# In-degree additions on VectorE at the start of the layers, and the copy of x plus offset written during the encoder

## Chip, core and metric

One core of a Trainium2 chip runs the whole kernel in one launch. The metric is the device time of an execution in microseconds, median of the runs; lower is better. TensorE, VectorE (DVE), ScalarE (ACT) and GpSimd (POOL) each work through their own queue in order; SyncE (SP) issues transfers, and GpSimd and ScalarE issue some of their own.

## What is computed

1250 nodes with 1024 features, 20000 edges sorted by target. First a network with an encoder, three residual graph layers and a decoder, then two mean-aggregating layers:

```python
h = layernorm(x, ln_in_g, ln_in_b)
h = relu(h @ W1 + b1) @ W2 + b2                      # encoder, 1024 -> 512 -> 256
for i in range(3):                                   # residual layers
    z = h + segment_sum(h[src], dst)
    z = relu(z @ Wa[i] + ba[i]) @ Wb[i] + bb[i]
    h = h + relu(layernorm(z, ng[i], nb[i]))
x = _layernorm(x + layernorm(x + decoder(h), out_g, out_b))
deg_inv = 1 / max(in_degree, 1)                      # used by the two layers that follow
h = relu(x @ Ws0 + (segment_sum(x[src]) * deg_inv) @ Wn0 + b0)
out = _layernorm(x + (h @ Ws1 + (segment_sum(h[src]) * deg_inv) @ Wn1 + b1))
```

## The kernel before

The graph becomes a matrix A[source, target] of edge counts, kept in SBUF as 10 blocks of 128 source rows by 1254 targets (1250 and four spare columns), and every `segment_sum` is then a matrix product on TensorE. Most products are done with a high and a low part of each float32 operand (`mm3`, L112 to L115: three matmuls; `split_w` and `relu_split` make the two parts, the high one mostly on ScalarE, the low one on VectorE or GpSimd).

**Encoder (L404 to L572).** Five chunks of two row tiles each (`PCH`, `y_chunk`, `h_rows`). A chunk c has four quarters f of 128 hidden columns, each with 24 matmuls into one PSUM buffer of the tag "ps", of which there are four; two `h_rows` follow a chunk in the same ring. In between stand the transpositions of the next chunk's x tiles (`transpose_x`, L437), whose tiles have the tag "xs" with four buffers, and the edges: groups of five edge tiles make one-hot matrices (`one_hots`), TensorE multiplies them (L344), ScalarE copies the product into a window of A and the product's last column into `carry` (L349, L352), and GpSimd adds the carry to the first column of the next window:

```python
S.activation(A[:, :, dst], pa[g][:, :, :w], AF.Copy)
...
first_col = A[:, :, bass.ds(bases[g - 1][1], 1)]
G.tensor_add(first_col, first_col.bitcast(F32), carry[g - 1])
```

As the windows lie where register values say, ScalarE's copy of a group waits for GpSimd's addition of the group before. When all groups are done, VectorE adds the identity to the ten diagonal blocks of A (L566). On VectorE that stands ahead of `hf` (L483), the encoder's row tiles, and these release the PSUM buffers of `h_rows`.

**Residual layers (L576 to L785).** `agg` multiplies h by A (L638) in three column pieces of 384, 512 and 358 targets; ScalarE and VectorE take the result as `zh` and `zl` (L643, L644); `z1_chunk` multiplies by Wa and its `relu_split` gives `z1h` and `z1l`; `z2_rows` multiplies by Wb, normalizes a row tile (L668 to L675) and writes the new h in two parts, `h0h` on ScalarE (L676) and `h0l` on GpSimd (L677). `load_wab` splits the weights of a layer, with the low part on GpSimd.

Two side jobs run in the layers:

- *In-degrees.* `asum` is the sum of A's ten blocks: five additions on VectorE before the first aggregation (L733 to L735), four on GpSimd after the first layer's rows (L772). `degrees` (L586 to L595) sums it over the partitions in layer 1 and writes the reciprocals to DRAM.
- *x plus offset.* `load_xo` (L717 to L726) loads the decoder's offset row `ob` into all partitions, writes it to all ten tiles of `xo_d` in DRAM (one transfer of 5120 KB, issued by SP), and adds x to it by five accumulating transfers of about 1 MB and one small one, issued by GpSimd. The decoder reads `xo_d` as `vt` (L899).

What sets the order: the head of the encoder, the decoder's rows and the final layers are written out by hand (`manual_schedule`). Elsewhere, in the rest of the encoder and in the layers, a scheduler places the instructions of each engine from the program's order and its own estimates. Waits between engines come from tiles: a tile in a released buffer waits for the last users of that buffer.

Of the kernel before, what the change touches and what calls it, by code (L numbers as in the profile page):

```python
# [10 lines left out]
F32 = mybir.dt.float32  # L11
# [5 lines left out]
ALU = mybir.AluOpType  # L17
# [4 lines left out]
P = 128  # L22
N = 1250
NG = 4
NN = N + NG
NT = 10
D = 1024
# [28 lines left out]
def gz(t):  # L56
    return P if t < NT - 1 else N - (NT - 1) * P + NG
# [7 lines left out]
def tile_gnn(ctx, tc, x, es, vecs, W1, W2, b2, Wa, Wb, bb, ng, nb, Wd1, Wd2, bd2, og, ob,  # L65
             Ws0, Wn0, b0l, Ws1, Wn1, b1l, out):
    nc = tc.nc
    V, S, G, T = nc.vector, nc.scalar, nc.gpsimd, nc.tensor
# [9 lines left out]
    xg_d = dram.tile([NG, D], F32, name="xg_d")  # L78
    x1_d = dram.tile([NT, P, D], F32, name="x1_d")
    h1_d = dram.tile([NT, P, D], F32, name="h1_d")  # L80
    xo_d = dram.tile([NT, P, D], F32, name="xo_d")

    def bcast(ap, n):
        return bass.AP(tensor=ap.tensor, offset=ap.offset, ap=[[0, P], [1, n]])
# [27 lines left out]
    def mm3(ps, a_hi, a_lo, b_hi, b_lo, start, stop, go_on=False):  # L112
        T.matmul(ps, a_hi, b_hi, start=start, stop=False, skip_group_check=go_on)  # L113
        T.matmul(ps, a_hi, b_lo, start=False, stop=False, skip_group_check=go_on)  # L114
        T.matmul(ps, a_lo, b_hi, start=False, stop=stop, skip_group_check=go_on)  # L115

    def pst(name, tag="ps", dt=F32):
        return psp.tile([P, 512], dt, name=name, tag=tag)
# [46 lines left out]
    S1 = tc.alloc_tile_pool(name="S1", bufs=1, reuse_waits="tile")  # L165
# [4 lines left out]
    ne, o = NGR * GT, 2 * NGR * GT  # L170
# [7 lines left out]
    xs = {}  # L178
# [203 lines left out]
    def any_edges():  # L382

        with tc.If(flag > 0):
            acc = Ap.tile([P, NT, AW], F32, name="acc", tag="A")
            V.memset(acc, 0.0)
            scratch = [B1.tile([P, 8 * (PW + 2)], F32, name=f"g{s}", tag=f"h0{s}0", bufs=1) for s in "hl"] + spare
            general_adjacency(tc, psp, acc[:, :, :N], (esrc, est[:, ne:2 * ne]), ident, ones, x, A_g, xg_d, scratch)
            res = Ap.tile([P, NT, AW], F32R, name="A", tag="A")
            nc.sync.dma_start(res.bitcast(F32)[:, :, :NN], A_g)  # L390
        return res
# [6 lines left out]
    def new_h(i):  # L398
        return [[hpool.tile([P, 5, DB], F32R, name=f"h{i}{s}{j}", tag=f"h{s}{j}", bufs=2) for j in range(2)]
                for s in "hl"]  # L400
# [25 lines left out]
    def transpose_x(c, ks=(0, 2, 4, 6)):  # L426
        tiles = PCH[c]
        w = sum(gz(t) for t in tiles)
        if c not in h0:
            h0[c] = new_h0(c)  # L430
        hi, lo = h0[c]
        for k in ks:
            pt = pst("pt").rearrange("p (k c) -> p k c", c=PW)
            for i in range(2):
                for j, t in enumerate(tiles):
                    n = gz(t)
                    T.transpose(pt[:, i, j * P:j * P + n], xs[t][:n, (k + i) * P:(k + i + 1) * P], ident[:n, :n])  # L437
            gs = [vec[:, C_G + k + i:C_G + k + i + 1] for i in range(2)]
            for i, g in enumerate(gs):
                S.activation(hi[:, k + i, :w], pt[:, i, :w], AF.Copy, scale=g)  # L440
            for i, g in enumerate(gs):
                V.scalar_tensor_tensor(lo[:, k + i, :w], pt[:, i, :w], g, hi[:, k + i, :w].bitcast(F32),  # L442
                                       ALU.mult, ALU.subtract)
# [31 lines left out]
    def h_rows(t):  # L475
        n = gz(t)
        o = (t % 2) * P
        ps = pst("ps_h")
        for k in range(4):
            yh, yl = yt[t // 2, k // 2]  # L480
            mm3(ps[:n, :DB], yh[:, k % 2, o:o + n], yl[:, k % 2, o:o + n], W2h[:, k], W2l[:, k], k == 0, k == 3)
        i, j = t // 5, t % 5
        V.tensor_add(hf[i][:n, j], ps[:n, :DB], b2c[:n])  # L483
        S.activation(hh[i][:n, j], hf[i][:n, j], AF.Copy)
        G.tensor_sub(hl[i][:n, j], hf[i][:n, j], hh[i][:n, j].bitcast(F32))
# [57 lines left out]
        load_W2()  # L543
    for f in range(4):
        V.tensor_add(b1c[:, f:f + 1], first[f][:, PW:PW + 1], vec[:, C_B1 + f:C_B1 + f + 1])
    NC = len(PCH)
    SLOTS = 13
    for c in range(NC):
        if c == 1:
            A = any_edges()  # L550
        for f in range(4):
            slot = 4 * (c - 1) + f
            y_chunk(c, f, -(-(ET - n_ed) // (SLOTS - slot)) if 0 <= slot < SLOTS else 0)
            if f == 0 and c > 0:
                for t in PCH[c - 1]:
                    h_rows(t)
            if 0 < c < NC - 1:
                transpose_x(c + 1, (2 * f,))
# [3 lines left out]
            if slot == SLOTS - 1:  # L562
# [4 lines left out]
                with tc.If(flag > 0):  # L567
                    nc.sync.dma_start(A.bitcast(F32)[:, :, :NN], A_g)
    for t in PCH[NC - 1]:
        h_rows(t)  # L570
    B1.release()
    S1.release()  # L572

# [2 lines left out]
    asum = WD2.tile([P, NN], F32, name="asum", tag="wd2_3")  # L576
    C3 = tc.alloc_tile_pool(name="C3", bufs=1, reuse_waits="tile")
# [36 lines left out]
    def begin_layer(i):  # L614
        ngc, nbc = (B2.tile([P, DB], F32, name=nm_, tag=nm_, bufs=1) for nm_ in ("ngc", "nbc"))
        bbr = wraw()[0:1, :DB]
        bbl = wraw()[0:1, :DB]
        nc.sync.dma_start(bbr, bass.AP(tensor=bb.tensor, offset=bb.offset + i * DB, ap=[[DB, 1], [1, DB]]))
        split_w(bbr, bbc[0:1], bbl)
        nc.sync.dma_start(bbc[1:2].bitcast(F32), bbl)  # L620
        nc.sync.dma_start(ngc, bcast(ng[i], DB))
        loads["nb"] = nc.sync.dma_start(nbc, bcast(nb[i], DB))
        z = new_z(("zh", "zl")) + new_z(("z1h", "z1l")) if i else z_first + new_z(("z1h", "z1l"))
        L[i].update(vecs=(bbc, ngc, nbc), z=z)

    def new_z(names):
        return [[B2.tile([P, NN], F32R, name=f"{nm_}{k}", tag=f"{nm_}{k}") for k in range(2)] for nm_ in names]
# [18 lines left out]
    def z1_chunk(i, c):  # L646
        c0, w = CL[c]
        cs = slice(c0, c0 + w)
        zh, zl, z1h, z1l = L[i]["z"]
        wh, wl = L[i]["w"]  # L650
        for f in range(2):
            ps = pst("ps_z1")
            for k in range(2):
                mm3(ps[:, :w], wh[:, k, f * P:(f + 1) * P], wl[:, k, f * P:(f + 1) * P],
                    zh[k][:, cs], zl[k][:, cs], k == 0, k == 1)
            bias = vec[:, C_BA + 2 * i + f:C_BA + 2 * i + f + 1]
            relu_split(ps, w, bias, z1h[f][:, cs], z1l[f][:, cs], B2, 512, f == 0)
# [56 lines left out]
            V.tensor_sub(d[64:], d[64:], bdo[64:, fs])  # L714
            S.activation(bdo[64:, fs], d[64:], AF.Copy)

    def load_xo():  # L717

        o = C3.tile([P, D], F32, name="o", tag="wt")
        nc.sync.dma_start(o, bcast(ob, D))  # L720
        nc.sync.dma_start(xo_d.rearrange("t p f -> p t f"), o.unsqueeze(1).broadcast_to([P, NT, D]))
        rows = xo_d.rearrange("t p f -> (t p) f")
        for t in range(0, NT, 2):
            r0, r1 = t * P, min(N, t * P + 2 * P)
            G.dma_start(rows[r0:r1], x[r0:r1], accum_op=ALU.add, max_dma_last_dim=4 * D)
        G.dma_start(rows[N:NN], xg_d, accum_op=ALU.add, max_dma_last_dim=4 * D)  # L726

    z_first = new_z(("zh", "zl"))
    load_wab(1)
    load_wab(0)  # L730
    begin_layer(0)
    load_xo()
    V.tensor_add(asum, A[:, 0, :NN].bitcast(F32), A[:, 1, :NN].bitcast(F32))  # L733
    for t in range(2, 6):
        V.tensor_add(asum[:gz(t)], asum[:gz(t)], A[:gz(t), t, :NN].bitcast(F32))  # L735
    for t0, t1 in ((0, 8), (8, NT)):
        agg(0, 0, t0, t1)
# [1 line left out]
    for i in range(3):  # L739
        nh, nl = new_h(i)  # L740

        def rows(*ts):
            for t in ts:
                z2_rows(i, t, nh, nl)

        z1_chunk(i, 0)
        z1_chunk(i, 1)
        rows(0, 1)
        agg(i, 2, 0, 5, (0,))
        rows(2, 3)  # L750
        agg(i, 2, 5, NT, (0,))
        if i == 1:
            degrees()
            load_Wd2(2)
        rows(4)
        agg(i, 2, 0, NT, (1,))
        rows(5, 6)
        if i == 2:
            break
        z1_chunk(i, 2)  # L760
        hh, hl = nh, nl
        agg(i + 1, 0, 0, 4)
        rows(7, 8, 9)
        begin_layer(i + 1)
        agg(i + 1, 1, 0, 4)
        agg(i + 1, 0, 4, 7)
        agg(i + 1, 1, 4, 7)
        if i == 0:
            with tc.issue_after(loads["nb"].ins):
                nc.sync.dma_start(A_d, A.bitcast(F32)[:, :, :NN])  # L770
            for t in range(6, NT):
                G.tensor_add(asum[:gz(t)], asum[:gz(t)], A[:gz(t), t, :NN].bitcast(F32))  # L772
            load_wab(2)
            for k in range(2):
                load_Wd2(k)
        else:
            load_Wd1()
            load_Wd2(3)
            load_bdo()
        agg(i + 1, 0, 7, NT)  # L780
        agg(i + 1, 1, 7, NT)
# [352 lines left out]
    A, loaded = {}, []  # L1134
# [178 lines left out]
    for i in range(2):  # L1313
# [3 lines left out]
        rows = h1_d if last else x1_d  # L1317
# [339 lines left out]
```

## Time and profile before

| | us |
|---|---|
| median of three runs | 932.36 (931.75 to 932.67) |
| the profiled execution, device time | 934.92 |
| its span in the profile | 933.1 |
| encoder ends, first aggregation starts | 128.3 |
| first aggregation ends, first product with Wa | 144.5 |
| layer 1's first zl | 188.97 |
| matmuls of the degrees | 203.6 |

The lines of a timeline give the start, the duration (of all instructions that were merged, with their count at the end), the engine, the line of the source, the operation, the tile written and those read with their shapes, and in brackets how long the engine was idle before and what released it. "issue" means that no releaser shows. A table of stretches gives, for each stretch, the busy time of each engine with its number of instructions, the granted clock of TensorE (1.00 is full), the busy share of the transfer engines, and GB/s. A matmul's record overlaps the next one, so its pitch is shorter than its duration.

### The profile page before, as it was taken

The page shows a single profiled execution, that of the slowest core. Times are in us where ns is not written, and L with a number is a line of the kernel's source. Part 1 is how long each engine was busy: PE and PEld are TensorE (multiplying, and loading weights), DVE is VectorE, ACT ScalarE, POOL GpSimd, SP SyncE. Part 2 cuts the span into 40 slices and gives each one's busy share as a digit, 9 for nine tenths or more (in the row PEclk, how much of TensorE's full clock was granted, in tenths as well). Part 3 has the DMA queues.
Part 4 walks back from the last instruction along what each step waited for, and adds up shares of the span by engine and source line. Part 5 has one row for each costly group of instructions (what it writes and reads, how often), then busy time and mean ns, then how long its engine had stood idle before and what let it go on. Part 6 is the DMA issues. An engine that isn't in the chain of part 4 may idle for free.

```text
span 933.1 us, 13196 instructions
## 1 busy us (share of the span) xinstructions
PE 898.3 (96%) x4753; PEld 790.0 (85%) x4759; DVE 646.2 (69%) x1269; ACT 393.7 (42%) x760; POOL 138.0 (15%) x160
## 2 busy tenths in 40 slices
PE   6789998999899999999999999999999999999997
PEld 4689998898887778999988888889999988888885
DVE  8878668676796774585677576455566786777785
ACT  3567523344566884111233345553211333333454
POOL 3467546526120000000000000000000000000000
PEclk9989999999999999999999999999999999999999
DMA  6300038973213739987452235446996722222214
GB/s 228 128 24 19 2 118 238 228 283 95 71 66 114 237 129 335 377 294 270 153 190 79 80 117 176 154 173 216 310 313 215 229 84 77 81 77 79 79 47 174
DMA packets 84163, 148.37 MB, mean 159 GB/s; under 512 B 8280, under 2 KB 31851, under 8 KB 84090
## 3 DMA queue, kind: packets, MB, share of 16 engines
q1 hardware_dynamic: 77062, 126.90, 40.1%
q0 software_dynamic: 2816, 10.27, 4.5%
q10 hardware_dynamic: 4212, 10.27, 2.9%
q8 instruction: 39, 0.64, 0.3%
q14 instruction: 34, 0.28, 0.1%
HBM read 103.35 MB, written 49.21 MB: 163 GB/s over the span
## 4 chain that ended last, share of the span: by engine, by line
PE 85%; DVE 6%; ACT 1%; DMA 1%; issue 1%; POOL 1%; ACTq 0%; POOLq 0%; DVEq 0%; SPq 0%
PE ps_A L1210 20%; PE ps_m L115 14%; PE ps_m L113 14%; PE ps_m L114 14%; PE ps_z L638 4%; PE ps_dd L113 2%; PE ps_dd L115 2%; PE ps_dd L114 2%; PE pa L344 2%; PE ps_y L113 2%; PE ps_y L114 2%; PE ps_y L115 1%; DVE z L673 1%; DVE hf L675 1%; PE pt L962 1%
## 5 line engine op out<-in xcount | busy, mean ns | idle before, releaser
L113 PE MATMUL ps_m<-w,th 128*128 128x512 f32 x520 | 204.0, 392 | 0.0
L115 PE MATMUL ps_m<-w,th 128*128 128x512 f32 x520 | 202.6, 390 | 0.0
L114 PE MATMUL ps_m<-w,th 128*128 128x512 f32 x520 | 202.3, 389 | 0.0
L1210 PE MATMUL ps_A<-A,qh 128*128 128x418 f32 (+1 forms) x480 | 170.6, 355 | 0.0
L1210 PE MATMUL ps_A<-A,ql 128*128 128x418 f32 (+1 forms) x480 | 169.9, 354 | 0.0
L115 PEld LDWEIGHTS ps_m<-w,th 128*128 128x128 f32 x520 | 97.6, 188 | 20.7
L114 PEld LDWEIGHTS ps_m<-w,th 128*128 128x128 f32 x520 | 97.7, 188 | 20.0
L113 PEld LDWEIGHTS ps_m<-w,th 128*128 128x128 f32 x520 | 97.6, 188 | 19.6
L1210 PEld LDWEIGHTS ps_A<-A,ql 128*128 128x128 f32 (+1 forms) x480 | 90.7, 189 | 1.9
L125 DVE TENSOR_TENSOR w<-stage,w 128x512 fp32r<-128x512 f32 x65 | 44.7, 691 | 67.9 <-ACT w L124 67.5
L1210 PEld LDWEIGHTS ps_A<-A,qh 128*128 128x128 f32 (+1 forms) x480 | 90.3, 188 | 1.4
L124 ACT ACTIVATE w<-stage 128x512 fp32r<-128x512 f32 x65 | 40.7, 629 | 118.7 <-PE ps_m L115 74.6
L1215 DVE TENSOR_TENSOR MT<-ps_A,dgb 128x418 f32<-128x418 f32 x48 | 25.5, 587 | 64.2 <-PE ps_A L1210 64.2
L1171 ACT ACTIVATE qh<-qraw 128x1280 fp32r<-128x1280 f32 (+3 forms) x28 | 21.5, 809 | 105.1 <-PE ps_A L1210 87.5
L113 PE MATMUL ps_y<-h0h,w1h 128*128 128x256 f32 (+2 forms) x160 | 54.9, 343 | 0.0
L125 DVE TENSOR_TENSOR w<-wraw,w 128x512 fp32r<-128x512 f32 x39 | 26.9, 689 | 32.8 <-ACT w L124 30.7
L114 PE MATMUL ps_y<-h0l,w1h 128*128 128x256 f32 (+2 forms) x160 | 46.4, 290 | 1.0 <-DVE h0l L442 1.0
L1299 DVE TENSOR_TENSOR c<-ps_m,c 128x512 f32<-128x512 f32 (+1 forms) x65 | 40.9, 683 | 8.8 <-PE ps_m L115 8.7
L115 PE MATMUL ps_y<-h0h,w1l 128*128 128x256 f32 (+2 forms) x160 | 46.1, 288 | 0.0
L1040 ACT ACTIVATE th<-XT 128x640 fp32r<-128x640 f32 x48 | 34.2, 725 | 20.5 <-DVE MT L1215 20.5
L124 ACT ACTIVATE w<-wraw 128x512 fp32r<-128x512 f32 x39 | 24.5, 629 | 41.9 <-PE ps_m L115 21.3
L328 POOL TENSOR_SCALAR Q<-iq,q 128x260 bf16<-128x260 f16 x31 | 37.9, 1223 | 14.6 <-PE pa L344 13.9
(306 smaller groups left out, 1897.9 us busy)
## 6 DMA issues: line engine op xcount, KB each, us to landing
A<-A_d SPq DMA_DIRECT2D x20, 627.0 KB
w_d<-stage SPq DMA_DIRECT2D x43, 256.0 KB
stage<-w_d SPq DMA_DIRECT2D x43, 256.0 KB
stage<-in_l_W_neigh_dram SPq DMA_DIRECT2D x42, 256.0 KB
stage<-in_l_W_self_dram SPq DMA_DIRECT2D x28, 256.0 KB
A_d<-A SPq DMA_DIRECT2D x1, 6270.0 KB
wraw<-in_l_W_neigh_dram SPq DMA_DIRECT2D x22, 256.0 KB
w_d<-wraw SPq DMA_DIRECT2D x21, 256.0 KB
```

Of the source, the lines that this page charges most:

```text
L113: T.matmul(ps, a_hi, b_hi, start=start, stop=False, skip_group_check=go_on)
L114: T.matmul(ps, a_hi, b_lo, start=False, stop=False, skip_group_check=go_on)
L115: T.matmul(ps, a_lo, b_hi, start=False, stop=stop, skip_group_check=go_on)
L124: S.activation(hi, raw, AF.Copy)
L125: return eng.tensor_sub(lo, raw, hi.bitcast(F32))
L328: G.tensor_scalar(q[:, 0], iq[:, :m], q4[:, g:g + 1], None, ALU.is_equal)
L638: T.matmul(ps[:, :w], hx[t // 5][:n, t % 5, f * P:(f + 1) * P], A[:n, t, c0:c0 + w], start=(t == 0 and s == 0), stop=(t == NT - 1 and s == 1))
L1040: S.activation(hi, src, AF.Copy)
L1171: S.activation(q[0][:, t0:t1], raw[:, t0:t1], AF.Copy)
L1210: T.matmul(pss[j][c][:, :w], qs[j][s][:n, t], A_of(t)[:n, c0:c0 + w], start=start and s == 0, stop=stop and s == 1)
L1215: V.tensor_mul(MT[:, f, c0:c0 + w], pss[j][c][:, :w], dgb[:, c0:c0 + w])
L1299: V.tensor_add(c, ps[:n], c if last or M in (6, 7) else c11[:n, t])
```

## The change

`load_xo` moves from the start of the residual layers to the end of the encoder, right after the last `h_rows`; the tile of the offset takes an x buffer (tag "xs") in place of one of the decoder's. The additions for blocks 6 to 9 of `asum` move from GpSimd, after layer 0's rows, to VectorE, in one row with the other five before the first aggregation.

```diff
@@ -543,6 +543,17 @@
         load_W2()
     for f in range(4):
         V.tensor_add(b1c[:, f:f + 1], first[f][:, PW:PW + 1], vec[:, C_B1 + f:C_B1 + f + 1])
+    def load_xo():
+
+        o = S1.tile([P, D], F32, name="o", tag="xs", bufs=4)
+        nc.sync.dma_start(o, bcast(ob, D))
+        nc.sync.dma_start(xo_d.rearrange("t p f -> p t f"), o.unsqueeze(1).broadcast_to([P, NT, D]))
+        rows = xo_d.rearrange("t p f -> (t p) f")
+        for t in range(0, NT, 2):
+            r0, r1 = t * P, min(N, t * P + 2 * P)
+            G.dma_start(rows[r0:r1], x[r0:r1], accum_op=ALU.add, max_dma_last_dim=4 * D)
+        G.dma_start(rows[N:NN], xg_d, accum_op=ALU.add, max_dma_last_dim=4 * D)
+
     NC = len(PCH)
     SLOTS = 13
     for c in range(NC):
@@ -568,6 +579,7 @@
                     nc.sync.dma_start(A.bitcast(F32)[:, :, :NN], A_g)
     for t in PCH[NC - 1]:
         h_rows(t)
+    load_xo()
     B1.release()
     S1.release()
 
@@ -714,24 +726,12 @@
-    def load_xo():
-
-        o = C3.tile([P, D], F32, name="o", tag="wt")
...
     z_first = new_z(("zh", "zl"))
     load_wab(1)
     load_wab(0)
     begin_layer(0)
-    load_xo()
     V.tensor_add(asum, A[:, 0, :NN].bitcast(F32), A[:, 1, :NN].bitcast(F32))
-    for t in range(2, 6):
+    for t in range(2, NT):
         V.tensor_add(asum[:gz(t)], asum[:gz(t)], A[:gz(t), t, :NN].bitcast(F32))
     for t0, t1 in ((0, 8), (8, NT)):
         agg(0, 0, t0, t1)
@@ -768,8 +768,6 @@
         if i == 0:
             with tc.issue_after(loads["nb"].ins):
                 nc.sync.dma_start(A_d, A.bitcast(F32)[:, :, :NN])
-            for t in range(6, NT):
-                G.tensor_add(asum[:gz(t)], asum[:gz(t)], A[:gz(t), t, :NN].bitcast(F32))
             load_wab(2)
             for k in range(2):
                 load_Wd2(k)
```

In the built program the scheduler puts the six accumulating issues on GpSimd's queue among the last five carry additions of the edges, ahead of the encoder's last four row tiles, and the offset's load and write on SP's queue behind the last x tiles. The nine additions stand in one row on VectorE, with one small subtraction between them, and GpSimd's queue holds none.

More of the change, by code (lines that the diff above doesn't have):

```diff
@@ L715, in load_bdo @@
             S.activation(bdo[64:, fs], d[64:], AF.Copy)
-    def load_xo():
-        o = C3.tile([P, D], F32, name="o", tag="wt")
[L720 to L726, printed above, removed]
     z_first = new_z(("zh", "zl"))
```

## Prediction

> **What bounds the kernel now.** I read the page first, then tables of two-microsecond stretches from 60 to 262 us, the timelines of GpSimd, VectorE and TensorE there, and the waits of TensorE from 120 to 215 us. The page says that TensorE is busy 96% of the span; a change off TensorE can only give or take at its holes.
>
> ```profile
> span 933.1 us, 13196 instructions
> ...
> PE 898.3 (96%) x4753; PEld 790.0 (85%) x4759; DVE 646.2 (69%) x1269; ACT 393.7 (42%) x760; POOL 138.0 (15%) x160
> ```
> Two holes lie where the change works. The table of stretches (us; busy time with number of instructions for PE, PEld, DVE, ACT, POOL; granted clock; DMA share; GB/s):
> ```profile
> 150.00:152.00 2.00, 0.51 (x2) 0.30 (x2) 1.97 (x2) 0.00 (x0) 1.92 (x2) 1.00 0.32 60
> 152.00:154.00 2.00, 0.77 (x6) 0.77 (x7) 1.79 (x3) 0.69 (x1) 2.00 (x3) 1.00 0.21 71
> ...
> 156.00:158.00 2.00, 2.00 (x9) 2.00 (x9) 2.00 (x8) 0.46 (x2) 0.00 (x0) 0.50 1.04 207
> ...
> 172.00:174.00 2.00, 1.06 (x6) 0.66 (x4) 2.00 (x5) 0.75 (x2) 1.02 (x2) 1.00 1.08 217
> ...
> 176.00:178.00 2.00, 2.00 (x11) 2.00 (x11) 1.67 (x6) 0.29 (x1) 0.00 (x0) 0.50 1.07 212
> ```
> Hole 1 is 2.81 us idle from 148 to 154 us (0.09+1.49+1.23), hole 2 1.6 us from 168 to 176 (0.07+0.07+0.94+0.54), and the clock is halved after each. Why, from VectorE's timeline (start, duration, instruction, count, idle before):
> ```profile
> 128.80 1.46 DVE L733 TENSOR_TENSOR asum<-A 128x1254 f32<-128x1254 f32 x1
> 130.29 9.60 DVE L735 TENSOR_TENSOR asum<-asum,A 128x1254 f32<-128x1254 f32 x3
> ...
> 147.44 3.06 DVE L154 CAST z1h<-ysp 128x384 fp32r<-128x384 f32 x1
> ...
> 168.46 3.65 DVE L673 SCALAR_TENSOR_TENSOR z<-z,rs,nbc 128x256 f32<-128x256 f32 x2
> ```
> The cast takes 0.35 us elsewhere (195.09) and the pair 0.87 (156.96). They are slow exactly while GpSimd runs its four additions, and five h0l in a row:
> ```profile
> 141.72 11.04 POOL L772 TENSOR_TENSOR asum<-asum,A 128x1254 f32<-128x1254 f32 x4 [4.66 <-issue]
> 152.71 2.99 POOL L725 DMA_DIRECT2D xo_d<-in_x_dram  x3
> 161.04 0.90 POOL L725 DMA_DIRECT2D xo_d<-in_x_dram  x1 [5.34 <-issue]
> 166.01 0.89 POOL L725 DMA_DIRECT2D xo_d<-in_x_dram  x1 [4.07 <-issue]
> 166.57 1.12 POOL L726 DMA_DIRECT2D xo_d<-xg_d  x1
> 167.10 3.42 POOL L677 TENSOR_TENSOR h0l<-hf,h0h 128x256 fp32r<-128x256 f32 x4
> ```
> Three accumulating transfers issue at once; GpSimd then stands still 5.34 and 4.07 us until the fourth and fifth can go. h0h was there at 158.95, its h0l starts at 167.10: the hold stops whatever is queued on GpSimd. At the place to which the issues move, VectorE's timeline has:
> ```profile
> 115.43 1.10 DVE L566 TENSOR_TENSOR A<-A,ident 128x128 fp32r<-128x128 f32 x5 [3.22 <-POOL A L355]
> 116.45 0.42 DVE L483 TENSOR_TENSOR hf<-ps_h,b2c 128x256 f32<-128x256 f32 x1
> ```
> VectorE adds the identity to A only after GpSimd's last carry (115.19 to 115.40), and the row tile hf stands behind that.
>
> **What the Trainium skill says.** SBUF — State Buffer, section "SBUF: two separate sides": VectorE (with two SBUF inputs or in a two-port mode) and GpSimd take one port pair as an exclusive lock for a whole instruction. The trace agrees: one asum addition alone is 1.45 us, three beside GpSimd 9.60. TensorE: Matmul & The Clock Gate, "What's actually happening": after an idle window of about 3.4 us the array runs at half rate, until a busy window. Here 0.50 stands after both holes, for some 3.4 us each, even though neither hole filled such a window. DMA: Bandwidth & Descriptors, "SWDGE vs HWDGE vs iDMA": accumulation can only be issued by GpSimd, which writes descriptors into rings. It does not say that a full ring holds GpSimd; the two idle times above do.
>
> **The change, part by part.**
>
> *Issues on GpSimd.* The built order puts them among the last five carry additions (109.52, 110.68, 112.93, 114.51, 115.19 now; c1 to c5): c1, D1, c2, D2, D3, D4, c3, D5, the small one, c4, c5. D1 waits for the broadcast write of the offset. That write's load needs the buffer of x tile 6, free after the last transposition (88.24+0.60 = 88.8). The load is an estimate of 3.5 us (two x tiles of its size, issued at 67.42, had moved by 72); the write, issued at 134.94 now, runs at 410 GB/s until 148.7, 13.8 us. So it lands near 107, and D1 goes at 109.7 behind c1, with 2.7 us to spare. From D1 I take the present spacing: D4 after 8.3 (161.04-152.71) at 118.0, D5 after 13.3 at 123.0, GpSimd free after 14.4 (167.10-152.71) at 124.1. Bounds: the holds could shrink to nothing (five issues at about 1 us), or everything slides with a later write.
>
> *Who stands behind it.* c3 runs at 118.6, c4 at 124.1. ScalarE's copies of the last two groups into A (L349) each wait for the carry before, as both write A: the first at 118.8, and behind it the relu of the last chunk's first quarter, done near 120.1; the second at 124.3. Then c5 at 124.7 and VectorE's identity at 125.0: 9.6 us late. TensorE has four PSUM buffers in that ring: the third quarter (119.66 now) waits 0.5 us for that relu, the fourth (122.34) for hf at 116.87+9.6 = 126.5. That is 3.7 us idle, 4.2 late. So idle, the clock should halve: of the quarter's 2.7 us I double 1.2. It ends at 130.4; relu, cast and subtraction (0.45+0.28+0.40 and their gaps) end at 131.65 instead of 126.43. The residual layers start 5.2 us late: 133.5 instead of 128.3. Bounds 3.5 (no clock loss) and 6.5.
>
> *Additions on VectorE.* Five become nine: 9x1.45 plus 0.41 (L125 between them) = 13.5 us. GpSimd's own work there (one hil 0.74, four wabl 1.27 each: 5.8) takes turns with it. That sum for now gives 0.5+7.7+5.8 = 14.0 us after the layer's start; measured 13.3 (141.59-128.29). Afterwards 0.5+13.5+5.8-0.7 = 19.1. The first zl, now starting at 14.4 and needed at 16.55, ends at 19.7 (0.56 for it): TensorE idles 3.2 us there, and loses 1.7 us to the half clock. The cover, 16.4 us of aggregation, holds only without GpSimd's part. In exchange hole 1 goes: no addition runs beside z1h. Hole 1 cost 2.8 and about 1.7 (3.4 us at half rate). Net +0.4, between -1.5 and +1.5.
>
> *GpSimd in the layer.* Four additions and the six issues leave it. Each h0l follows its h0h at once and takes its turn with VectorE singly, with VectorE's idle moments (1.1 us at 164.6) to absorb it. Hole 2 cost 1.6 and some 1.7 of clock; I leave 0.9 of it, as the same five h0l still take their turns. With small waits for h0l from 169 to 171 (0.4): -2.8, between -3.7 and 0.
>
> *Moved on SP.* Two issues go ahead of the layer's loads; the 5 MB write no longer lies before them. bbc and Wa land sooner, but nothing waited on them on the path: 0. The one vt load moved forward on GpSimd waits for D2, landed by then: 0. The degrees are used at 203 us: 0.
>
> Sum: +5.2 +0.4 -2.8 = +2.8. The profiled execution took 934.92 us, span 933.1 and 1.8 around it; it lies 2.56 above the median of 932.36. Against its own time the sum gives 937.7; against the median 935.2. I say 935.2, as the later 730 us are TensorE's own and carry a shift along.
>
> **Rivals.** *Faster: the holds don't recur.* One mechanism: if the two waits come from VectorE's activity at 155 to 166 us and not from the drain, then beside an idle VectorE the five issues pass in about 5 us, c5 ends some 2 us late, and hf still precedes 122.34. That has 5.4 us of slack (122.34-116.87), so it decides there: a hold under 5.4 us costs nothing, over it TensorE pays. Then +0.4-2.8 = -2.4: 930.0. For it: no view names what those two waits waited for. Against: D4 and D5 go 8.3 and 13.3 us after D1, in step with 1 MB at 207 GB/s each.
>
> *Much slower: the write is late, or the adds wait longer.* If the offset's write lands 3 us or more after 109.7, every carry slides along, one for one; +3 to +5 on top: about 939. For it: only 2.7 us to spare, on an estimated load. Against: the stretches from 72 to 126 us show at most 8 GB/s on the queues.
>
> *Traded evenly:* a hold of 7 us instead of 9.6 costs TensorE 2.6 less and nearly cancels: 932.6. That the change does not do what it says is excluded by the built order: nine additions on VectorE, none on GpSimd, six issues before the layer.
>
> **Numbers.** Forecast 0.55, much slower 0.17, even 0.08, faster 0.20. The forecast's own range takes its three bounds, not all at one end: 932.5 to 938.5. Within 0.2%, about what a measurement of this kernel can tell from no change, is 930.5 to 934.2: 0.3 of the forecast's chance (0.16), the even case and 0.02 of the faster one lie there. So slower 0.39+0.17 = 0.56, same 0.26, faster 0.18. The range leaves out half of the faster case below and half of the much slower one above: 929.3 to 939.3.
>
> **What would show it.** Right: idle GpSimd of about 5 and 4 us between its issues at 113 to 123 us; ScalarE's L349 waiting for GpSimd; the identity near 125; the layer starting near 133.5; a hole before the first zl; casts of z1h at 0.35 us; the half clock after the second chunk gone. Wrong: the identity before 121, a first zl not late, or the 168 us pair still at 3.6 us.

## The result and the profile after

The changed kernel takes 936.53 us in the median of 7 runs (934.52 to 937.87), the kernel before on the same chip 932.67 (931.75 to 934.73): a ratio of 1.0032, 95% interval 1.0021 to 1.0044. It is slower by 2 to 4 us. The prediction said 935.2, slower, 2.8 us.

The page of the changed kernel begins (engine, busy time, share, number of instructions):

```profile
span 934.7 us, 13199 instructions
...
PE 896.6 (96%) x4759; PEld 789.4 (84%) x4759; DVE 644.4 (69%) x1273; ACT 393.9 (42%) x760; POOL 125.7 (13%) x156
```

GpSimd is 12 us less busy (138.0 before), and the span is 1.6 us longer. TensorE's waits from 100 to 200 us (total, number, longest) name two large ones that the kernel before did not have (and 0.3 us for ysp); its own waits there, 3.3 us for z1l and 1.0 for z1h, are gone:

```profile
PE ps_y L113 <- DVE hf L483: 3.9, 1, 3.9
PE ps_z L114 <- DVE zl L656: 3.3, 1, 3.3
```

The first comes from GpSimd's timeline (start, duration, instruction, count, idle time before it):

```profile
109.25 0.20 POOL L355 TENSOR_TENSOR A<-A,carry 128x10 f32 x1
109.40 1.12 POOL L554 DMA_DIRECT2D xo_d<-in_x_dram  x1
110.43 0.46 POOL L355 TENSOR_TENSOR A<-A,carry 128x10 f32 x1
110.83 1.78 POOL L554 DMA_DIRECT2D xo_d<-in_x_dram  x2
117.64 0.90 POOL L554 DMA_DIRECT2D xo_d<-in_x_dram  x1 [5.03 <-issue]
118.22 0.56 POOL L355 TENSOR_TENSOR A<-A,carry 128x10 f32 x1
122.60 0.89 POOL L554 DMA_DIRECT2D xo_d<-in_x_dram  x1 [3.82 <-issue]
...
125.00 0.21 POOL L355 TENSOR_TENSOR A<-A,carry 128x10 f32 x1 [0.46 <-ACT A L349]
```

The two holds moved along with the issues: 5.03 and 3.82 us here, 5.34 and 4.07 in the layer before. The carries wait behind them, and two engines wait for the carries. ScalarE:

```profile
118.81 0.59 ACT L349 ACTIVATE A<-pa 128x500 f32 x1 [6.16 <-POOL A L355]
...
124.57 0.35 ACT L349 ACTIVATE A<-pa 128x210 f32 x1 [4.76 <-POOL A L355]
```

VectorE, with the additions that follow:

```profile
125.24 1.10 DVE L577 TENSOR_TENSOR A<-A,ident 128x128 fp32r<-128x128 f32 x5 [13.30 <-POOL A L355]
126.26 0.42 DVE L483 TENSOR_TENSOR hf<-ps_h,b2c 128x256 f32<-128x256 f32 x1
...
136.35 9.61 DVE L735 TENSOR_TENSOR asum<-asum,A 128x1254 f32<-128x1254 f32 x3
145.88 0.41 DVE L125 TENSOR_TENSOR wraw<-wraw,bbc 1x256 f32<-1x256 f32 x1
146.21 7.45 DVE L735 TENSOR_TENSOR asum<-asum,A 128x1254 f32<-128x1254 f32 x5
153.57 2.21 DVE L656 TENSOR_TENSOR zl<-ps_z,zh 128x384 fp32r<-128x384 f32 x4
...
158.47 0.36 DVE L154 CAST z1h<-ysp 128x384 fp32r<-128x384 f32 x1 [0.56 <-ACT ysp L150]
```

The cast that took 3.06 us beside GpSimd's additions takes 0.36, but zl now starts at 153.57 (142.65 before, with a layer that began 6.1 us earlier). In the table of stretches (busy time and number for PE, PEld, DVE, ACT, POOL; clock; DMA share; GB/s) both new holes bring the half clock, and hole 2 is gone:

```profile
124.00:126.00 2.00, 0.00 (x0) 0.00 (x0) 0.76 (x4) 0.63 (x2) 0.75 (x3) 1.00 1.07 213
126.00:128.00 2.00, 1.27 (x6) 1.27 (x7) 2.00 (x9) 0.42 (x1) 0.80 (x1) 0.67 1.05 207
128.00:130.00 2.00, 2.00 (x11) 2.00 (x11) 1.52 (x5) 1.50 (x4) 1.10 (x2) 0.50 1.07 213
...
152.00:154.00 2.00, 0.00 (x0) 0.00 (x0) 1.97 (x3) 0.00 (x0) 0.00 (x0) 0.99 0.00 0
154.00:156.00 2.00, 1.82 (x6) 1.82 (x7) 1.78 (x4) 0.00 (x0) 0.00 (x0) 0.50 0.00 0
156.00:158.00 2.00, 2.00 (x9) 1.95 (x8) 0.56 (x1) 1.25 (x3) 0.00 (x0) 0.65 0.03 8
...
176.00:178.00 2.00, 2.00 (x15) 2.00 (x14) 2.00 (x5) 0.68 (x3) 0.78 (x1) 1.00 0.02 4
```

Two stretches hold nearly all of the change. *Encoder's end* runs from the start of GpSimd's last one-hot (L328, last in order before the copy) to the start of VectorE's last hf (102x256), *layer 0* from there to ScalarE's first relu of layer 1 (first 128x384 ysp). Each is one profiled execution, in us; the medians are over all runs, as differences from the kernel before on the same chip:

| kernel | encoder's end | layer 0 | sum against before | median against before |
|---|---|---|---|---|
| before | 20.0 | 65.1 | | |
| after | 26.3 | 60.8 | +2.0 | +3.9 |
| e1, copy moved alone | 27.7 | 60.5 | +3.1 | +4.0 |
| e2, additions moved alone | 20.0 | 62.7 | -2.5 | -1.3 |
| e3, after, ring 2880 | 20.0 | 64.9 | -0.3 | -0.2 |
| e4, after, copy behind the carries | 20.0 | 68.4 | +3.3 | +4.1 |
| e5, e3 with L125 behind the additions | 20.0 | 59.5 | -5.7 | -2.5 |
| e6, before, late additions | 20.0 | 61.6 | -3.5 | -1.7 |
| e7, e6 with ring 2880 | 20.0 | 55.6 | -9.5 | -4.7 |
| e8, after, ring 1024 | 46.7 | 60.9 | +22.5 | +22.9 |
| e9, early copy, late additions, ring 2880 | 20.0 | 56.2 | -8.9 | -8.0 |
| e10, e7 again | 20.0 | 56.1 | -9.0 | -3.7 |

The sums lie up to 3.2 us below the medians, and 5 us for e7 and e10, where something is given back later. Each row is one execution, and executions differ. The one of before, the reference of the sums, took 934.92 us, 2 us over its median; the start of its last one-hot, 108.32, lies between 106.65 and 109.89 us in all twelve. After a hole of the same length at the same place the half clock lasts longer in one than in another: e1 and after have the same edit in the encoder and the same wait there, 3.92 us, but the time from the end of that wait to the layer's start is 8.62 us in e1 and 7.46 in after, and in e5 no half clock follows at all. A sum is thus good to some 2 or 3 us, and the medians decide.

### The profile page after: what moved, and what is told of

Same layout as the page of the kernel before. It is cut to its first block, busy times and chain, and to the rows that moved or that the text cites. A ratio compares the mean times of both kernels' runs of the same rounds, so it can differ in the third digit from the quotient of the medians.

```text
span 934.7 us, 13199 instructions
## 1 busy us (share of the span) xinstructions
PE 896.6 (96%) x4759; PEld 789.4 (84%) x4759; DVE 644.4 (69%) x1273; ACT 393.9 (42%) x760; POOL 125.7 (13%) x156
## 4 chain that ended last, share of the span: by engine, by line
PE 81%; DVE 6%; issue 3%; POOL 2%; ACT 1%; DMA 1%; POOLq 0%; ACTq 0%; DVEq 0%; SPq 0%
PE ps_A L1208 20%; PE ps_m L115 14%; PE ps_m L113 14%; PE ps_m L114 14%; PE ps_z L650 3%; PE ps_dd L113 2%; PE ps_dd L115 2%; PE ps_dd L114 2%; DVE asum L735 2%; PE pa L344 1%; PE ps_y L113 1%; PE ps_z L115 1%; PE ps_z L114 1%; PE pt L960 1%; PE ps_y L114 1%
## 5 line engine op out<-in xcount | busy, mean ns | idle before, releaser
L125 DVE TENSOR_TENSOR w<-stage,w 128x512 fp32r<-128x512 f32 x65 | 44.7, 691 | 67.9 <-ACT w L124 67.6
L1213 DVE TENSOR_TENSOR MT<-ps_A,dgb 128x418 f32<-128x418 f32 x48 | 25.5, 586 | 64.9 <-PE ps_A L1208 64.9
L125 DVE TENSOR_TENSOR w<-wraw,w 128x512 fp32r<-128x512 f32 x39 | 26.9, 689 | 32.8 <-ACT w L124 32.6
L328 POOL TENSOR_SCALAR Q<-iq,q 128x260 bf16<-128x260 f16 x31 | 38.0, 1226 | 14.5 <-PE pa L344 13.7
```

Of the source, the lines that this page charges most:

```text
L125: return eng.tensor_sub(lo, raw, hi.bitcast(F32))
L328: G.tensor_scalar(q[:, 0], iq[:, :m], q4[:, g:g + 1], None, ALU.is_equal)
L1213: V.tensor_mul(MT[:, f, c0:c0 + w], pss[j][c][:, :w], dgb[:, c0:c0 + w])
```

## The experiments

Theory from the prediction: the holds on GpSimd delay the encoder's end and the layer; moving the additions is an even exchange; freeing GpSimd in the layer is a gain. Rival: the loss comes from the additions, or the holds cost nothing because other work covers them. The medians are set against the kernel before on the same chip: 933.16 us for e1 to e4, 932.40 for e5 to e8, 933.33 for e9 and e10.

### One part alone

e1 moves load_xo as the change does and leaves the last four additions on GpSimd.

```diff
     for t in PCH[NC - 1]:
         h_rows(t)
+    load_xo()
...
     begin_layer(0)
-    load_xo()
```

> Only the copy of x plus offset moves into the encoder; the four additions stay on GpSimd. Theory (GpSimd's hold between the issues costs, the nine additions cost nothing net): TensorE's wait for hf of 3.9 us stays and the layers start about 6 us late as in the changed kernel; the hole behind z1h and z1l of some 2.8 us stays as in the kernel before; the hole near 173 us is gone, worth 4.4. Sum about +1.7 us against the kernel before, 0.1 to 0.4% slower. Rival (the nine additions are what makes the changed kernel slower): 2 to 4 us faster than before.

937.16 us, ratio 1.0042 (1.0029 to 1.0055). TensorE waits 3.9 us for hf as in the changed kernel, and 2.2 and 0.7 us for z1l and z1h as in the kernel before. The copy alone makes the kernel slower, by 4.0 us where 1.7 were expected; the encoder's end carries all of it (7.7 us, of which the longer half clock is 1.2 more than in the changed kernel), and in layer 0 it gives back 4.6 us: hole 2.

e2 moves the additions alone.

```diff
-    for t in range(2, 6):
+    for t in range(2, NT):
         V.tensor_add(asum[:gz(t)], asum[:gz(t)], A[:gz(t), t, :NN].bitcast(F32))
...
-            for t in range(6, NT):
-                G.tensor_add(asum[:gz(t)], asum[:gz(t)], A[:gz(t), t, :NN].bitcast(F32))
```

> Only the four additions move to VectorE; the copy stays in the layers. Theory: the layers start on time, the first zl is late and TensorE waits for it 3.3 us, which takes the place of the hole behind z1h (net +0.1 us); the issues stand on GpSimd some 3 us earlier than before, so h0l is held less and the second hole shrinks. Sum -1 us, between 0 and -3. Rival (the additions cost): +2 to +3 us.

931.85 us, ratio 0.9983 (0.9975 to 0.9990). The wait for zl is there (3.3 us), hole 1 is not. The small gain, expected at 1 us and measured at 1.3, has another source: without additions ahead of them the issues on GpSimd start at 147.9 instead of 152.7 (3.1 us earlier once the encoder's end, 1.7 us earlier in this execution, is taken off), its holds end 2.0 us earlier on the same count, and hole 2 shrinks to a wait of 0.5 us for z1l. From the first product with h0h to the 128x512 one it is 9.89 us before, 6.05 in e2 and 5.33 in e1: either part of the change alone takes away most of hole 2, so the gains of the two parts don't add up.

### The holds taken away

e3 is the changed kernel with a larger descriptor ring (bytes per partition); e8 has a smaller one.

```diff
-    nc = _bacc.Bacc("TRN2", target_bir_lowering=False, num_devices=1, dynamic_dma_scratch_size=2048)
+    nc = _bacc.Bacc("TRN2", target_bir_lowering=False, num_devices=1, dynamic_dma_scratch_size=2880)
```

> The changed kernel with descriptor space of 2880 instead of 2048 bytes per partition, nothing else. Theory (the fourth and fifth issue wait for space in the ring): all five issues pass in about 5 us, no idle GpSimd of 5.0 and 3.8 us between them, VectorE's identity within 2 us of 115.2 instead of 125.2, no wait for hf; the two other terms stay (+0.1 and -4.4). About 4 us faster than the kernel before, 6 to 8 us faster than the changed kernel. Rival (they wait for the first transfers to land whatever the space): as the changed kernel, +2 to +3 us.

932.95 us, ratio 0.9997 (0.9986 to 1.0007): the kernel before again, where 4 us less were expected. The holds are gone: all issues lie between 108.6 and 115 us, the encoder's end is as before to 0.1 us. But layer 0 takes 64.9 us instead of 60.8. TensorE's waits in e3:

```profile
PE ps_z L114 <- DVE zl L656: 6.3, 1, 6.3
```

e4 keeps the ring and puts the copy behind the last carry.

```diff
-            G.tensor_add(first_col, first_col.bitcast(F32), carry[g - 1])
+            last_carry = G.tensor_add(first_col, first_col.bitcast(F32), carry[g - 1])
...
-    load_xo()
+    with tc.issue_after(last_carry.ins):
+        load_xo()
```

> The changed kernel with the six issues queued behind GpSimd's last carry addition. Theory (the hold costs only through the carries that stand behind it): the holds stay at about 5 and 4 us but lie at 123 to 129 us, where only the parts hil of the last row tiles stand behind them, which are needed from 130 us on; identity at 115.2, layers start on time; about 4 us faster than the kernel before. Rival (the hold costs wherever it stands, or the traffic of the transfers does): +2 us or more.

937.28 us, ratio 1.0047 (1.0033 to 1.0061): slower where 4 us of gain were expected. The holds (3.70 and 4.80 us) cost the encoder nothing, and TensorE waits 8.3 us for zl and 1.3 for zh. In e3 and e4 alike, the removed wait was replaced by a longer one, in the layer. Its cause shows on ScalarE in e3:

```profile
139.87 0.63 ACT L124 ACTIVATE wabh<-wraw 128x512 fp32r<-128x512 f32 x1 [10.69 <-DMA wraw<-in_layer_Wb_dram]
140.41 0.40 ACT L124 ACTIVATE bbc<-wraw 1x256 fp32r<-1x256 f32 x1
```

and on VectorE in e3:

```profile
129.23 8.62 DVE L735 TENSOR_TENSOR asum<-asum,A 128x1254 f32<-128x1254 f32 x3
140.90 1.24 DVE L125 TENSOR_TENSOR wraw<-wraw,bbc 1x256 f32<-1x256 f32 x1 [3.05 <-ACT bbc L124]
142.07 7.45 DVE L735 TENSOR_TENSOR asum<-asum,A 128x1254 f32<-128x1254 f32 x5
```

The copy's transfers keep the DMA share near or over 1 from about 112 to 138 us in e3. With the layer now starting at 127 instead of 134, they lie beside its loads: ScalarE waits 10.69 us for Wb, bbc stands behind it, and VectorE's small bias operation, between the fourth and the fifth addition, waits 3.05 us for bbc; five additions and zl wait behind it. From its issue on SP to ScalarE's use of it, this load of Wb takes 8.8 us in e3 (131.06 to 139.87) and 2.8 before (131.44 to 134.20) and after (138.19 to 140.98). In e4, where the transfers start later, the same chain gives a wait of 14.31 us for Wb and one of 4.18 for bbc. The DMA page of the Trainium skill (DMA: Bandwidth & Descriptors, "Issuing engines are not separate DMA queues") says that transfers issued by any engine end up on the same 16 DMA engines and interleave; these waits agree.

To test that chain, e5 is e3 with this one operation behind the ninth addition. As an operation can only be put behind one that is already written, `begin_layer(0)` moves behind the first part of the aggregation in the program; the loads of ngc and nbc go at 109 instead of 124 us with it.

```diff
-        split_w(bbr, bbc[0:1], bbl)
+        S.activation(bbc[0:1], bbr, AF.Copy)
+        with tc.issue_after(loads["add"].ins):
+            V.tensor_sub(bbl, bbr, bbc[0:1].bitcast(F32))
...
-    begin_layer(0)
...
-        V.tensor_add(asum[:gz(t)], asum[:gz(t)], A[:gz(t), t, :NN].bitcast(F32))
+        loads["add"] = V.tensor_add(asum[:gz(t)], asum[:gz(t)], A[:gz(t), t, :NN].bitcast(F32))
...
         agg(0, 1, t0, t1)
+        if t0 == 0:
+            begin_layer(0)
```

> The changed kernel with the larger descriptor ring (2880), and with VectorE's one small operation of the bias row (1x256, the lower half of bb) put behind the ninth addition instead of between the fourth and the fifth; nothing is left out. Theory (in the run with the larger ring alone, that operation waited 3.05 us for ScalarE's bbc, which waited for the load of Wb behind the accumulating transfers, and took 1.24 us instead of 0.41; all additions after it and the first zl were late by that): the additions run through, first zl some 18.7 us after the first addition starts (21.7 with the larger ring alone), TensorE's wait for it falls from 6.3 back to 3.3 us, and the time is 3.0 us under that of the larger ring alone: 930.0 us. Rival (the transfers slow the layer's start in another way, such as ScalarE's zh behind the late Wb): the wait stays at 5 us or more and the time at 932 to 933 us.

929.94 us, ratio 0.9968 (0.9958 to 0.9979), 930.0 expected. VectorE in e5:

```profile
129.84 17.09 DVE L738 TENSOR_TENSOR asum<-asum,A 128x1254 f32<-128x1254 f32 x8
146.85 0.41 DVE L633 TENSOR_TENSOR wraw<-wraw,bbc 1x256 f32<-1x256 f32 x1
147.19 2.20 DVE L659 TENSOR_TENSOR zl<-ps_z,zh 128x384 fp32r<-128x384 f32 x4
```

From the first addition (128.35) to zl it is 18.8 us, 21.7 in e3 and 18.7 in the changed kernel; TensorE's wait is back at 3.4. ScalarE still waits 10.74 us for Wb in e5, and its first zh comes at the same distance from the first addition (13.3 us in both), so the late Wb does not delay TensorE in another way. The 3 us that e3 waits more were that one operation of 1x256, in a row of additions that had no use for it.

e8, the smaller ring:

```diff
-    nc = _bacc.Bacc("TRN2", target_bir_lowering=False, num_devices=1, dynamic_dma_scratch_size=2048)
+    nc = _bacc.Bacc("TRN2", target_bir_lowering=False, num_devices=1, dynamic_dma_scratch_size=1024)
```

> The changed kernel with a smaller descriptor ring (1024); nothing is left out. Theory (GpSimd stands still until the ring has room, so its hold grows as the ring shrinks; a transfer takes some 4.2 us, and half the ring holds about two transfers fewer): the last carry comes some 8.5 us later, the fourth quarter's wait for hf grows from 3.9 to about 12 us, and the time is 944 to 946 us. Rival (the hold is tied to something other than the ring's room, such as the write of the offset): within 1 us of the changed kernel, 936.5 us.

955.34 us, ratio 1.0237 (1.0214 to 1.0261): the direction as expected, twice the size. GpSimd in e8:

```profile
108.20 1.12 POOL L554 DMA_DIRECT2D xo_d<-in_x_dram  x1
...
116.96 0.92 POOL L554 DMA_DIRECT2D xo_d<-in_x_dram  x1 [7.27 <-issue]
125.00 0.89 POOL L554 DMA_DIRECT2D xo_d<-in_x_dram  x1 [7.12 <-issue]
133.09 0.90 POOL L554 DMA_DIRECT2D xo_d<-in_x_dram  x1 [7.21 <-issue]
...
141.47 0.89 POOL L554 DMA_DIRECT2D xo_d<-in_x_dram  x1 [7.25 <-issue]
```

One transfer is out at a time, every 8.1 us, and not every 4.2 as I had reckoned with the transfers still overlapping. The fifth goes at 141.47 instead of 122.60, 18.9 us later, and the medians differ by 18.8 (955.34 - 936.53). Rings of 1024, 2048 and 2880 admit one, three and all five large transfers at once. The hold is the ring's room.

### Additions where VectorE is idle

e6 is the kernel before, with its last four additions on VectorE behind layer 0's last hf, where VectorE had been idle 6.5 us. e7 adds the larger ring.

```diff
-        V.scalar_tensor_tensor(h, z2[:n], 0.0, h, ALU.max, ALU.add)
+        loads["hf"] = V.scalar_tensor_tensor(h, z2[:n], 0.0, h, ALU.max, ALU.add)
...
-            for t in range(6, NT):
-                G.tensor_add(asum[:gz(t)], asum[:gz(t)], A[:gz(t), t, :NN].bitcast(F32))
+            with tc.issue_after(loads["hf"].ins):
+              for t in range(6, NT):
+                V.tensor_add(asum[:gz(t)], asum[:gz(t)], A[:gz(t), t, :NN].bitcast(F32))
```

> The kernel before, the copy of x left in the layer, and its last four additions given to VectorE behind the last hf of layer 0, where it stood idle 6.5 us; nothing is left out. Theory (the hole of the kernel before came from GpSimd's additions slowing VectorE's z1h and z1l; moved to an idle stretch they cost nothing, while all nine at the start cost a wait of 3.3 us for zl): no wait for z1l or z1h and none for zl, the second hole as in the run with the additions moved alone (1.5 us) or as before, 4.5 us under before: 928 us (927 to 929.5). Rival (the additions only move the wait: they hold up layer 1's first zl, or the transfers now issued earlier do the same to z1l): 931 us or more.

930.72 us, ratio 0.9975 (0.9963 to 0.9987), short of the 928 expected. No wait for zl, and of those for z1l and z1h 0.9 us is left; but hole 2 has grown. GpSimd takes up h0l at 167.28 (167.10 before), behind the holds, while the first hf is there at 155.6 instead of 157.7 although this execution's encoder ended 1.4 us later, and TensorE now waits for h0l outright (e6's waits):

```profile
PE ps_z L638 <- POOL h0l L677: 3.4, 1, 3.4
```

> As the run before it (the kernel before, last four additions on VectorE behind layer 0's last hf), with the larger descriptor ring (2880). Theory: GpSimd does not stand still among its issues, h0l is on time, and the second hole goes too: 1.5 to 3 us under the run before it, 925 to 926.5 us. Rival (the second hole is TensorE's wait for something else, or traffic over the layer slows loads): the same time as the run before it.

927.73 us, ratio 0.9941 (0.9920 to 0.9963): 3.0 us under e6, at the upper end of what was expected of the step, but over the 925 to 926.5 expected, since e6 began higher. In layer 0 TensorE now has no wait at all; in layer 1 it waits 3.8 us for zh (0.6 before).

### Early copy or late copy

e9 is e5 with the last four additions late as in e6 (the bias operation stands behind the fifth addition): the early copy with every wait found so far taken away. e10 runs e7 again beside it.

```diff
-    for t in range(2, NT):
+    for t in range(2, 6):
...
+            with tc.issue_after(loads["hf"].ins):
+                for t in range(6, NT):
+                    V.tensor_add(asum[:gz(t)], asum[:gz(t)], A[:gz(t), t, :NN].bitcast(F32))
```

> The copy as early as in the changed kernel, with the larger ring (2880), the last four additions on VectorE behind layer 0's last hf, and the bias row's small operation behind the first five additions; nothing is left out. Theory (the change's early place for the copy is worth nothing by itself: what it gained in the layer it gained by freeing GpSimd, and the larger ring does that at either place): within 1 us of the run with late additions, larger ring and the copy left in the layer, both near 927.7 us. Rival 1 (traffic of 27 us beside the layer's inputs still costs): 929 us or more. Rival 2 (the early place helps by itself): under 926 us.

925.37 us, ratio 0.9914 (0.9899 to 0.9929).

> The same kernel as in the run with late additions and the larger ring (the copy of x left in the layer), beside the run with the early copy on the same chip: 927.7 us again (927 to 928.5).

929.66 us, ratio 0.9957 (0.9943 to 0.9972): over the 928.5 expected at most, but as a ratio inside the interval of e7, the same kernel on another chip. My theory, that the early place by itself is worth nothing, fell: the intervals of e9 and e10, run side by side, don't meet (those of e9 and e7 do). Their encoder's end and layer 0 are equal (table), so the difference is later. TensorE's waits in e10:

```profile
PE ps_z L113 <- ACT zh L643: 5.4, 1, 5.4
```

It stands at 209 us, in layer 1. In e9 it is 0.8 us, so most of the 4.3 us between the medians is this wait. ScalarE in e10, where zh is the last line:

```profile
203.23 0.63 ACT L124 ACTIVATE wd<-wraw 128x512 fp32r<-128x512 f32 x1 [5.43 <-DMA wraw<-in_Wd_dram]
...
208.03 0.63 ACT L124 ACTIVATE wd<-wraw 128x512 fp32r<-128x512 f32 x1 [2.64 <-DMA wraw<-in_Wd_dram]
208.57 0.40 ACT L676 ACTIVATE h1h<-hf 128x256 fp32r<-128x256 f32 x1
208.87 0.45 ACT L643 ACTIVATE zh<-ps_z 128x358 fp32r<-128x358 f32 x1
```

In e10 the write of A (to A_d, 6270 KB) is issued at 174.5, while the late copy still runs: the DMA share stays near 1 from 154 to 202, the decoder's Wd rows come behind both, and ScalarE stands still for them with zh in its queue. In e9 the copy is over by 142, and the DMA share falls at 198. In the kernel before the write goes at 182.6, when the copy is over, layer 1 is 8 us later than in e10, and TensorE waits 0.6 us for zh. So the gain in layer 0 has moved layer 1 onto transfers that it used to miss. This is read from the traces; no run moves the write of A by itself.

e9 is 0.86% faster than the kernel before on the same chip.

## Why the prediction held, and where it was off

The sign was right, the time lies in the range, and both losses came where and how the prediction said. That the sum came so close was partly luck: the encoder's term was 1.1 us too small and the gain on GpSimd 1.6 us too small, and the two errors pull opposite ways. By its steps (in single executions, as above):

*Issues on GpSimd.* Predicted D4 at 118.0, D5 at 123.0; measured 117.64 and 122.60, with D1 at 109.40, the offset's write over by 106. The hold could be carried over to another place because it belongs to the ring and the transfers' rate, not to what VectorE does beside it: rings of three sizes show it (e8, after, e3). That answers the faster rival: the holds recur beside a VectorE that stands idle for 13.30 us. The prediction took the spacing over without knowing its cause; the cause came with e3 and e8.

*Who stands behind it.* VectorE's identity: 125.0 predicted, 125.24 measured; the fourth quarter's wait 3.7, measured 3.92. The term was +5.2 and measured +6.3 (26.3 - 20.0). Of the 1.1 us, 0.5 is the quarter's start (counted from the last one-hot, 4.7 later instead of 4.2) and 0.5 the half clock: I doubled 1.2 us of the quarter; from its start to the layer's it took 7.46 us instead of 5.78, 1.7 more (in e1, after the same wait, 2.8 more). The rest is what I rounded between them.

*Additions on VectorE.* +0.4 predicted. TensorE's wait 3.3 (3.2), half clock 1.5 to 1.7 (0.50 in one stretch of 2 us and 0.65 in the next, 1.0 + 0.7; or 6.28 - 4.83 us by the table at the end). From the layer's start to the first product of the third chunk (zh with wabh, 128x358) it is 38.56 us before and 38.65 after: +0.1. An even exchange it was, within a us: in e2, where the half clock after the same hole lasts longer, the same distance is 39.78. In e6, which has the additions in neither place, it is 33.63, so each place costs about 5 us, where the prediction had 4.5 and 4.9. e9 against e5, which differ in the place of the last four additions, gives 5.0 us in the medians (0.9968 - 0.9914 = 0.0054 of 933).

*GpSimd in the layer.* The term that was mis-sized: -2.8 predicted, -4.4 measured (from the first h0h product to the 128x512 one 9.89 us before, 5.53 after), -4.6 in e1. I held 0.9 us back for h0l in a row beside VectorE's pair. Each h0l now comes singly behind its h0h (165.61, 167.16, 169.49), and the two instructions of the pair take 0.48 each: nothing of hole 2 was left. Another 0.4 lies in the 16 products with A at the head of the stretch, 3.63 us before and 2.81 after, of which I had counted 0.4; 0.3 stays open.

*Moved on SP: 0* (two issues go ahead of the layer's loads). Right for the changed kernel: ScalarE's wait for Wb is 4.67 us (3.96 before), and VectorE's L125 waits for nothing. But it was right only because the layer started late: the transfers ended near 137, 3 us after the layer's start. Where the layer starts on time, as in e3, the step is worth 3.0 us, and in e4 more. My expectations for e3 and e4 fell on the same step, since I had looked for what GpSimd's issues hold up and not for what the transfers hold up once issued.

Sum of the terms in the profile +2.0, in the medians +3.9; predicted +2.8. The 1.9 us between the first two are about what the profiled execution of before lies over its median (2.3); in which stretch that excess lies is not shown.

Left open: by what rule room in the ring is given back, which no view shows; one, three and five transfers in 1024, 2048 and 2880 fit a transfer that takes between 512 and 576 bytes per partition, an inference. Larger rings were not run. The halvings of the clock were read off the stretches and not varied by themselves.

## What to carry to other kernels

A queue on which an engine both computes and issues transfers can stand still for as long as the transfers take: before moving issues onto it, count what stands behind them, and see whether the issuing engine already stands still at the old place, because the hold moves along. When a hold is removed, ask next which loads the transfers now lie beside, and which instruction at the head of a row waits for such a load; a 1x256 subtraction in the wrong place of VectorE's row cost 3 us here. Moving a transfer early paid (4 us between e9 and e10) only once the ring's holds, the bias operation and the additions were out of its way.

## What the runs showed of the hardware

GpSimd's wait at an accumulating transfer depends on the descriptor ring: 7.2 us at each of four issues with 1024 bytes per partition, 5.0 and 3.8 us at two with 2048 (changed kernel), none with 2880. With 1024 the DMA share falls to 0.02 between two transfers, and the first five issues spread over 33 us instead of 13.

The half clock did not follow a hole's length. TensorE waits for the first zl at the same place of the same work in four runs; from the end of that wait to the first product with z1h it takes

| run | wait, us | clock in the stretches of 2 us after it | to the first product with z1h, us |
|---|---|---|---|
| e5 | 3.4 | 1.00 throughout | 4.83 |
| after | 3.3 | 0.50, 0.65 | 6.28 |
| e2 | 3.3 | 0.50, 0.50, 0.50 | 7.38 |
| e3 | 6.3 | 0.50, 0.50, 0.59 | 7.36 |

```profile
148.00:150.00 2.00, 2.00 (x12) 2.00 (x12) 1.39 (x3) 1.01 (x2) 0.00 (x0) 1.00 0.05 9
```

(e5, right behind its wait.) The Trainium skill (TensorE: Matmul & The Clock Gate, "What's actually happening") calls the window of about 3.4 us free-running; that a hole of like length pays in one execution and not in another agrees with it, but no run here varies the phase. A hole of about 3 us at this place thus cost between its own length and some 2.6 us more (7.38 - 4.83), not the fixed 1.7 that the prediction added.
